# Attention and non-local block: where the sums of the nested products run, and in which order image 0 is prepared

## The chip, the cores and the metric

The kernel runs on one core of one Trainium2 chip. A core has TensorE (matrix products into PSUM, called PE in the profile, with PEld for its weight loads), VectorE (DVE), ScalarE (ACT), GpSimd (POOL), SyncE (SP, which here only issues transfers) and 16 DMA engines. Times are device microseconds (us) of a run; the median over runs is what is compared. The profile is of one more execution.

## The reference

For 8 images x of 512 channels and 32 x 32 positions, in float32:

```
q, k, v = Wq x + bq, Wk x + bk, Wv x + bv          # 1x1 convolutions, 8 heads of 64 channels
attn    = softmax(q^T k / 8)                       # over 1024 keys, per head
x       = x + Wp (attn v) + bp
g, th, ph = Wg x + bg, Wtheta x + btheta, Wphi x + bphi   # 256 channels each
f       = th ph^T / 1024                           # 256 x 256
z       = Ww (f g) + bw + x
out     = (z - mean) * rsqrt(var + 1e-5) * gamma + beta   # per channel, over all images and positions
```

## The kernel before

The function `unshifted` does all the work; `shifted` follows only if a denominator of the softmax is not sane. The channels lie on partitions, in four blocks of 128; an image is a tile of 128 x 4 x 1024.

**Order of the work.** A loop runs over the images b. Its body is: `attention(b)`; then q, v and k of image b+1, in this order, by `heads_of` and `values`; then the projection Wp of image b (`project`); theta and phi (`theta_phi`); and the non-local part (`nonlocal_`: g, f, their product with Ww, z, and the statistics). Image 0's q, k and v come ahead of the loop, in the order q, k, v.

**Products in seven.** Every large product is computed as seven products of half-size blocks in place of eight (a Winograd form). For this the data x = (11, 12; 21, 22) needs sums t1 to t4 (`more_sums`: t1 = 12 - 11, t2 = 22 - t1, t3 = 22 - 12, t4 = 21 - t2) and the weights need sums w3 to w6 (`weight_sums`). `seven` does one such product; its table SEVEN gives each of the seven its weight block, its data block, its PSUM bank and which quarters of the result read it.

**Nested products.** For q, k and v of images 1 to 7 six of the seven outer products are again done in seven (`six`): this needs inner sums of each data block (`inner_parts`, four instructions of 128 x 256 each) and of each weight block (`inner_weights`, kept in DRAM after image 0). The six come as three pairs (SIX): pair 0 gives the quarter 11 and a part of 12, pair 1 gives 22 and a temporary T6, pair 2 a temporary T7 and 21. A pair has seven steps, each with one product for either member. In a step a PSUM bank is read by ACT where the piece is the first of its quarter (`write`), else by DVE, which adds PSUM to the piece in SBUF. The seventh outer product (`plain`, 11 x 11) is done whole between pair 1 and pair 2. ACT copies it to a temporary T1, with the bias, which is then added to T6 and 11. The rest are sums of whole quarters (`add`, 128 x 1024, both operands in SBUF): for q and k, T6 += T1, 11 += T1, 12 += T6, 12 += 22, T7 += T6, 22 += T7, 21 += T7, all on GpSimd; for v two of them on DVE.

**PSUM.** There are four tiles of two banks each; `next_bank` takes the one longest unused. Pair n takes four: two for the products of steps 0, 2, 4 and 6, two for those of steps 1, 3 and 5. The plain product takes one.

**What fills the gaps.** `six` takes `fills`, work of DVE to be put behind a given step of a pair or ("middle") ahead of the plain product. In q these are t3 and t4 of the next image, their inner sums and the softmax's denominators (a reciprocal on DVE, which reads PSUM); in v the four products o x 1/denominator (L677), two on GpSimd and two on DVE; in k the sums t1 to t4 of o (L252) and the inner sums of o's quarter 21; after k those of o's t4. In attention `near_end` puts t1, t2 and four inner sums of x between the steps of the list AT.

**Queues.** `pe`, `dve` and `sp` are one helper, keep_in_program_order: the instruction is placed behind the one written just before it on its engine. Instructions without it are placed by a planner. At run time every engine takes its own in order[...]. So the place of a GpSimd sum in the text orders it against other GpSimd work, not against DVE.

**Image 0.** Its weights come from the inputs; their sums are formed and written to DRAM (`keep`, `keep_inner`). The projection of image 0 is not nested: `weights("WpT")` has no inner sums yet; they are formed after it (L1083), and w3 to w6 of theta/phi in `weights("tp")`. ngamma, dq and dk (differences of biases, used with T7) are formed after q of image 0 (L983 to L986).

Of the kernel before, what the change touches and what calls it, by code (L numbers as in the profile page):

```python
# [8 lines left out]
F32 = mybir.dt.float32  # L9
# [21 lines left out]
def unshifted(ctx: ExitStack, tc: tile.TileContext, a: dict, out: bass.AP):  # L31
# [154 lines left out]
    def weights(name, sums_done=False, pin=lambda ins: None):  # L186

        w = loaded.pop(0)
        assert w.name == name
        if name not in kept:  # L190
            if not sums_done:
                weight_sums(w, corner[name], pin=pin)
            keep("plain" if name == "WpT" else name, w)
        return w
# [51 lines left out]

    def more_sums(data, which, pin=lambda ins: None):
        for i in which:
            l, r = {1: ("12", "11"), 2: ("22", "t1"), 3: ("22", "12"), 4: ("21", "t2")}[i]
            if f"t{i}" not in data:  # L250
                data[f"t{i}"] = block(f"t{i}_{data['name']}")
            pin(nc.vector.tensor_tensor(data[f"t{i}"], data[l], data[r], ALU.subtract))  # L252

# [3 lines left out]

    def inner_parts(data, which, pin=lambda ins: None):
# [5 lines left out]
        return [lambda i=i, l=l, r=r: pin(nc.vector.tensor_tensor(t[:, i], l, r, ALU.subtract))  # L264
                for i, (l, r) in enumerate(((b12, b11), (b22, t[:, 0]), (b22, b12), (b21, t[:, 1])))]
# [85 lines left out]

    def six(name, w, data, positions_out, at, write, fills):

# [19 lines left out]
        def plain():  # L373
            ps = next_bank(f"{name}_0")
            d = data["11"]
            if positions_out:
                ps = ps.rearrange("p h (i f) -> p (h i) f", f=256)
            for i in range(4 if positions_out else 2):
                for k in range(2):
                    if positions_out:  # L380
                        pe(nc.tensor.matmul(ps[:, i, :], d[:, k, i * P:(i + 1) * P], w[:, 0, k, :],  # L381
                                            start=(k == 0 and i % 2 == 0), stop=(k == 1), skip_group_check=True))
                    else:
                        pe(nc.tensor.matmul(ps[:, i, :], w[:, 0, k, i * P:(i + 1) * P], d[:, k, :],
                                            start=(k == 0), stop=(k == 1), skip_group_check=True))
            if positions_out:
                nc.scalar.copy(to("T1"), ps)
            else:
                for i in range(2):
                    write("T1", i, to("T1")[:, i, :], ps[:, i, :])  # L390
            load_w("first")
            add("T6", "T1", nc.vector if positions_out else nc.gpsimd)
            if not positions_out:
                add("11", "T1")
            add("12", "T6")

        for n, pair in enumerate(SIX):
# [7 lines left out]
            for step, which in enumerate(ORDER):  # L405
                _, wi, di, chain, reads = SEVEN[which]
                for m, (outer, of, q) in enumerate(pair):
                    a, d = w.inner(outer)[wi], data[f"inner {of}"][di]
                    ps = slots[m if not chain else 2 + m][:, chain // 2, :256]
                    start = (m, chain) not in begun  # L410
                    begun.add((m, chain))
                    if positions_out:
                        ps = ps.rearrange("p (i f) -> p i f", f=P)
                        for i in range(2):
                            pe(nc.tensor.matmul(ps[:, i, :], d[:, i * P:(i + 1) * P], a, start=start and not i, stop=True,  # L415
                                                skip_group_check=True))
                    else:
                        pe(nc.tensor.matmul(ps, a, d, start=start, stop=True, skip_group_check=True))  # L418
                    for (i, j), is_first in reads:
                        i, j = int(i) - 1, int(j) - 1  # L420
                        if is_first:
                            write(q, i, piece(q, i, j), ps)
                        else:
                            dve(nc.vector.tensor_tensor(piece(q, i, j), piece(q, i, j), ps, ALU.add))  # L424
                for one in fills.pop((n, step), ()):
                    one()
            load_w()
            if n == 1:
                add("12", "22")
        assert not fills, fills  # L430
        if positions_out:
            add("11", "T1", nc.vector)
        add("T7", "T6")
        add("22", "T7")
# [67 lines left out]
    def heads_of(b, what, w, bias, data, pin=lambda ins: None, steps=None, fills=None, **how):  # L502
# [3 lines left out]
        if fills is not None:  # L506
            def write(q, i, to, ps):
                by = steps if q == "T7" else bias if q == "T1" else None
                if by is None:
                    nc.scalar.copy(to, ps)  # L510
                else:
                    nc.scalar.activation(to, ps, AF.Identity, bias=by[:, i:i + 1])

            six(f"p{what}_{b}", w, data, False, lambda q: t[:, rows(q), cols(q)], write, fills)
            return t
# [13 lines left out]
    def values(b, w, data, fills=None):  # L529
# [8 lines left out]
        if fills is not None:  # L538
            six(f"pv_{b}", w, data, True, at, lambda q, i, to, ps: nc.scalar.copy(to, ps), fills)  # L539
            return v  # L540
# [4 lines left out]
    def attention(b, q, k, v, near_end, make_f=None):  # L545
# [128 lines left out]
        def normalize(d):  # L674
# [14 lines left out]
            for k in range(2):  # L689
                for j in range(2):  # L690
                    sp(nc.sync.dma_start(r[j * D:(j + 1) * D, k, :], d[j, k].partition_broadcast(D)))
            r = r.rearrange("q k (p c m) -> q k c p m", p=NPAIR, c=2)
            return [lambda k=k, h=h: product(o["o"][:, :, h * 512 + k * 256:h * 512 + (k + 1) * 256], r[:, k, h],
                                            None if k else nc.gpsimd)
                    for k in range(2) for h in range(NH)]
# [286 lines left out]
    bv, bp, gb, wb, gamma, beta = (load_col(n, nc.sync) for n in ("bvc", "bp", "gb", "Wb", "gamma", "beta"))  # L982
    nc.vector.tensor_scalar(ngamma, gamma, -1.0, 1.0, ALU.mult, ALU.mult)  # L983
    dq, dk = (const.tile([P, CC // 2], F32, tag=n, name=n) for n in ("dq", "dk"))
    for to, of in ((dq, bq), (dk, bk)):
        nc.vector.tensor_tensor(to, of[:, CC // 2:], of[:, :CC // 2], ALU.subtract)  # L986
    weight_sums(wk, corner["WkT"], pin=dve)
# [9 lines left out]
    v = values(0, wv, data)  # L997
    aside_weights = [one for blocks in PAIRS for i in blocks for one in inner_weights(wv, i)]
    held = {}
    AT = (26, 29, *(33 + 8 * n // 5 for n in range(16)))  # L1000
    for b in range(B):
# [6 lines left out]
        if not last:  # L1008
            nxt["data"] = data_sums(quarters_of(nxt["x"]), f"x_{b + 1}", ())
            sums += [lambda i=i: more_sums(nxt["data"], (i,), dve) for i in (1, 2)]  # L1010

# [31 lines left out]
        if not last:  # L1043
            data = nxt["data"]
            t3, t4 = (inner_one_by_one(data, of) for of in ("t3", "t4"))
            q = heads_of(b + 1, "q", weights("WqT"), bq, data, dve, steps=dq, fills={
                (0, 6): [lambda: more_sums(data, (3,), dve)], (1, 0): [lambda: more_sums(data, (4,), dve)],
                (1, 6): t3[:2],
                "middle": [lambda: nxt.update(products=normalize(denominators(next_bank(f"den_{b}")))), *t3[2:], *t4]})
            products = nxt["products"]  # L1050
# [49 lines left out]
        tp = theta_phi(b, weights("tp"), data, tpb, {} if last else  # L1100
                       {5: lambda: b < B - 2 and of_theta.append(f_sums(b, tps[0], 0))})
        load_w("first")
# [247 lines left out]
```

## Time and profile before

Three runs took 2158.82 us at the median (2158.23 to 2159.34). The profiled execution took 2159.93 us; its span, in which instructions ran, is 2158.1 us. The mean clock granted to TensorE is 0.992 of full.

| what | number |
|---|---|
| busy PE / DVE / ACT / POOL, us of 2158.1 | 2105.4 / 1495.6 / 844.2 / 512.2 |
| attention of one image (1142.49 to 1252.51) | 110.02 |
| q, v, then k with the projection (to 1346.70) | 23.50, 22.29, 48.40 |
| theta/phi, then non-local (to 1404.70) | 24.14, 33.86 |
| POOL sum of 128x1024, L371, undisturbed | 2.36 |
| DVE sum of 128x1024, both operands in SBUF, L252 of x | 1.22 |
| the same, L252 of o (t_o), mean of 16 and 16 | 2.05 and 2.16 |
| DVE inner sum of 128x256, L264 of x / of t_o | 0.42 / 1.55 and 2.51 |
| DVE reading PSUM with one SBUF operand: L424 128x256, L603 128x512, L730 128x512 with bias | 0.42, 0.68, 0.74 |
| ACT T1, L512 128x512; T7's first piece, 128x256 | 0.68, 0.48 |

How to read it: a line of the timeline gives the start, the duration, the engine, the line of the kernel, the operation, what it writes and reads, and in brackets how long the engine had been idle and what released it. Ends of matmuls are modelled, and neighbouring ones overlap, so TensorE's gaps are better read from distances between starts. A row of windows gives the stretch, its length, the busy time of PE, PEld, DVE, ACT and POOL with their instructions, the clock granted to TensorE, and the share and rate of the DMA engines.

### The profile page before, as it was taken

Reading aid. Unit: us, or ns where it says so; the run is one execution under the profiler, and the core shown is the slowest. Engines: PE = TensorE matmul, PEld = TensorE weight load, DVE = VectorE, ACT = ScalarE, POOL = GpSimd, SP = SyncE. Lnnn points to the kernel's source line nnn. Section 1 sums busy time; section 2 is a strip of 40 time slices with the busy share of each in tenths; the row PEclk is TensorE's granted clock in tenths of the full one; section 3 lists DMA queues with packets and bytes.
Section 4 is the critical chain, followed back from the end, with each engine's and each line's share of the span. In section 5 each row is a group of like instructions: output and inputs, shape, how many; then the busy total and the mean of one; then the engine's idle time right before and its main releaser. Section 6 shows DMA issues by size and latency. Waiting matters only on the chain.

```text
span 2158.1 us, 33299 instructions
## 1 busy us (share of the span) xinstructions
PE 2105.4 (98%) x13486; PEld 1175.5 (54%) x13486; DVE 1495.6 (69%) x1935; ACT 844.2 (39%) x1220; POOL 512.2 (24%) x340
## 2 busy tenths in 40 slices
PE   9999989999999999999999999999999999999996
PEld 4535754358643577336673376633866348643462
DVE  5587856768677685776857768677684777656736
ACT  1365303653046530464205642066412654056116
POOL 0012800128001370014500155011630117111000
PEclk9999999999999999999999999999999999999998
DMA  6254533235232432325224252142534235212767
GB/s 224 81 143 84 174 123 114 40 79 154 98 108 40 103 126 98 115 38 135 88 98 118 41 152 98 66 123 40 164 122 152 40 57 158 86 30 40 229 221 314
DMA packets 71729, 243.56 MB, mean 113 GB/s; under 512 B 12688, under 2 KB 21136, under 8 KB 69520
## 3 DMA queue, kind: packets, MB, share of 16 engines
q1 hardware_dynamic: 60640, 215.01, 29.9%
q0 software_dynamic: 9072, 24.78, 9.3%
q8 instruction: 108, 1.77, 0.3%
q10 hardware_dynamic: 1856, 1.56, 0.3%
q14 instruction: 53, 0.43, 0.1%
HBM read 160.45 MB, written 47.32 MB: 96 GB/s over the span
## 4 chain that ended last, share of the span: by engine, by line
PE 84%; DVE 9%; DMA 3%; ACT 2%; issue 1%; SPq 0%; ACTq 0%; DVEq 0%; POOLq 0%
PE ps L571 20%; PE po L597 20%; PE ptp L340 8%; PE pv_in L415 6%; PE pq_in L418 5%; PE pp L340 4%; PE pg L340 4%; DVE t_o L252 3%; PE pz L340 3%; DVE i_t_o L264 2%; PE pf L792 2%; PE pp_in_s L297 2%; DVE k L424 1%; PE pv L381 1%; PE pv L340 1%
## 5 line engine op out<-in xcount | busy, mean ns | idle before, releaser
L574 ACT ACTIVATE e<-ps 128x1024 f32<-128x1024 f32 x512 | 523.0, 1025 | 427.5 <-PE ps L571 421.9
L580 DVE TENSOR_TENSOR acc<-acc,e 128x1024 f32<-128x1024 f32 x384 | 469.8, 1223 | 106.6 <-ACT e L574 100.6
L571 PE MATMUL ps<-q,k 64*64 64x512 f32 x4096 | 529.3, 589 | 0.0
L597 PE MATMUL po<-e,v 64*64 64x512 f32 x4096 | 528.6, 589 | 0.0
L610 POOL DMA_DIRECT2D fold<-acc x189 | 144.8, 766 | 1376.4 <-PE ps L571 707.8
L597 PEld LDWEIGHTS po<-e,v 64*64 64x64 f32 x4096 | 156.6, 133 | 282.9 <-issue 275.0
L571 PEld LDWEIGHTS ps<-q,k 64*64 64x64 f32 x4096 | 155.5, 133 | 283.5 <-issue 275.6
L835 ACT ACTIVATE g<-pg,gb 128x512 f32<-128x512 f32 x31 | 21.3, 687 | 467.8 <-PE pg L340 467.6
L578 DVE TENSOR_TENSOR acc<-e,e 128x1024 f32<-128x1024 f32 x64 | 78.3, 1224 | 127.9 <-ACT e L574 125.7
L340 PE MATMUL ptp<-w_tp,t_x 128*128 128x256 f32 x512 | 116.7, 383 | 6.3 <-DVE tp L757 4.6
L340 PEld LDWEIGHTS ptp<-w_tp,t_x 128*128 128x128 f32 x512 | 98.2, 192 | 21.0 <-DVE tp L757 5.4
L340 PE MATMUL pp<-t_o,w_WpT 128*128 128x512 f32 x208 | 103.5, 606 | 0.0
L340 PE MATMUL ptp<-w_tp,x 128*128 128x256 f32 x384 | 86.8, 379 | 0.0
L340 PEld LDWEIGHTS ptp<-w_tp,x 128*128 128x128 f32 x384 | 73.0, 190 | 13.3 <-issue 3.8
L424 DVE TENSOR_TENSOR v<-v,pv_in 128x256 f32<-128x256 f32 x84 | 34.8, 421 | 51.9 <-PE pv_in L415 50.9
L371 POOL TENSOR_TENSOR k<-k,T_pk 128x1024 f32<-128x1024 f32 x28 | 70.1, 2524 | 0.5
L340 PE MATMUL pp<-o,w_WpT 128*128 128x512 f32 x144 | 67.8, 593 | 2.3 <-DVE o L677 2.3
L763 DVE TENSOR_TENSOR tp<-tp,ptp 128x1024 f32<-128x1024 f32 x24 | 29.3, 1221 | 53.5 <-PE ptp L340 53.5
L371 POOL TENSOR_TENSOR q<-q,T_pq 128x1024 f32<-128x1024 f32 x28 | 65.4, 2356 | 0.5
L418 PE MATMUL pk_in<-i_t_x,w_WkT 128*128 128x256 f32 x224 | 57.3, 383 | 2.0 <-DVE k L424 1.2
L510 ACT COPY k<-pk_in 128x256 f32<-128x256 f32 x112 | 42.0, 375 | 44.3 <-PE pk_in L418 40.6
L539 ACT COPY v<-pv_in 128x256 f32<-128x256 f32 x112 | 41.8, 374 | 44.2 <-DVE T_pv L424 19.3
(231 smaller groups left out, 3038.7 us busy)
## 6 DMA issues: line engine op xcount, KB each, us to landing
fold<-acc POOLq DMA_DIRECT2D x189, 128.0 KB, 3.1
w_WqT<-kept_WqT SPq DMA_DIRECT2D x21, 896.0 KB, 4.5
w_WvT<-kept_WvT SPq DMA_DIRECT2D x21, 896.0 KB, 5.1
w_WkT<-kept_WkT SPq DMA_DIRECT2D x21, 896.0 KB, 5.8
r<-den_d SPq DMA_DIRECT2D x32, 512.0 KB, 6.9
x<-in_x_dram SPq DMA_DIRECT2D x30, 512.0 KB, 5.9
spill<-x SPq DMA_DIRECT2D x24, 512.0 KB, 4.0
z<-spill SPq DMA_DIRECT2D x24, 512.0 KB, 10.0
```

Source lines behind the costliest of these rows:

```text
L252: pin(nc.vector.tensor_tensor(data[f"t{i}"], data[l], data[r], ALU.subtract))
L340: pe(nc.tensor.matmul(to_ps, lhsT(k), rhs(k), start=(s, at) not in begun, stop=(k == nk - 1), skip_group_check=True))
L371: dve((engine or nc.gpsimd).tensor_tensor(to(q), to(q), to(of), ALU.add))
L415: pe(nc.tensor.matmul(ps[:, i, :], d[:, i * P:(i + 1) * P], a, start=start and not i, stop=True, skip_group_check=True))
L418: pe(nc.tensor.matmul(ps, a, d, start=start, stop=True, skip_group_check=True))
L424: dve(nc.vector.tensor_tensor(piece(q, i, j), piece(q, i, j), ps, ALU.add))
L571: pe(nc.tensor.matmul(ps[c * P // 2:(c + 1) * P // 2, j, :], k[r, p, keys], q[r, p, h * 512:(h + 1) * 512], start=True, stop=True, skip_gr ...
L574: nc.scalar.activation(e, ps, AF.Exp, scale=SCALE)
L578: nc.vector.tensor_tensor(accs[u], es[u, 0], e, ALU.add)
L580: ins = nc.vector.tensor_tensor(accs[u], accs[u], e, ALU.add)
L597: pe(nc.tensor.matmul(ps[j * D:(j + 1) * D, r, :], v[keys, m, (2 * p + j) * D:(2 * p + j + 1) * D], e[keys, j, :], start=(m == 0), stop=(m ...
L610: nc.gpsimd.dma_start(to, part_of, accum_op=ALU.add)
```

## The change

- `plain` is done in two halves, each in a bank of its own. DVE adds each half straight from PSUM to T6 and to 11 (`plus`, with the bias for q and k). T1 and its ACT copies are gone.
- T7's first pieces are read by DVE as PSUM + T6 (with dq or dk for q and k). T7 += T6 is gone.
- GpSimd has four sums per stage, for v too: 12 += 22 (now written after the plain product), 12 += T6, 22 += T7, 21 += T7.
- All four products o x 1/denominator are GpSimd's. So are o's t1 to t3 (written at the start of k) and the inner sums of o's t4. o's t4 and the inner sums of its 21 stand on DVE after pair 1 of k.
- x's t3 moves into attention, where AT starts at step 22; x's t4 and the inner sums of t3 and t4 stand around pair 1 of q, none in "middle".
- Image 0: dq, dk and ngamma come after v, pinned. Wp's inner sums go between the products of theta/phi, w3 to w5 of theta/phi stand ahead of it and w6 within it; the writes to DRAM and one load come after it.

```diff
@@ weights() @@
-        if name not in kept:
+        if name not in kept and name != "tp":
...
@@ more_sums() and, alike, inner_parts() @@
-            pin(nc.vector.tensor_tensor(data[f"t{i}"], data[l], data[r], ALU.subtract))
+            pin((engine or nc.vector).tensor_tensor(data[f"t{i}"], data[l], data[r], ALU.subtract))
@@ plain() @@
-            ps = next_bank(f"{name}_0")
...
-            if positions_out:
-                nc.scalar.copy(to("T1"), ps)
-            else:
-                for i in range(2):
-                    write("T1", i, to("T1")[:, i, :], ps[:, i, :])
+            for half in range(2):
+                ps = next_bank(f"{name}_0_{half}")[:, 0, :]
...
+                for q in ("T6", "11"):
+                    at_ = to(q)[:, half * 2:half * 2 + 2, :] if positions_out else to(q)[:, half, :]
+                    plus(at_, ps, at_, "first", half)
             load_w("first")
-            add("T6", "T1", nc.vector if positions_out else nc.gpsimd)
-            if not positions_out:
-                add("11", "T1")
+            add("12", "22")
             add("12", "T6")
@@ the pairs @@
-                        if is_first:
-                            write(q, i, piece(q, i, j), ps)
+                        if is_first and q == "T7":
+                            plus(piece(q, i, j), ps, piece("T6", i, j), "third", i)
+                        elif is_first:
+                            nc.scalar.copy(piece(q, i, j), ps)
...
-            if n == 1:
-                add("12", "22")
         assert not fills, fills
-        if positions_out:
-            add("11", "T1", nc.vector)
-        add("T7", "T6")
         add("22", "T7")
         add("21", "T7")
@@ heads_of() @@
+            def plus(to, ps, of, what, i):
+                by = bias if what == "first" else steps
+                dve(nc.vector.scalar_tensor_tensor(to, ps, by[:, i:i + 1], of, ALU.add, ALU.add))
@@ values() @@
-            six(f"pv_{b}", w, data, True, at, lambda q, i, to, ps: nc.scalar.copy(to, ps), fills)
+            six(f"pv_{b}", w, data, True, at, lambda to, ps, of, *_: dve(nc.vector.tensor_tensor(to, of, ps, ALU.add)), fills)
@@ normalize() @@
-                                            None if k else nc.gpsimd)
+                                            nc.gpsimd)
@@ image 0, after q and after v @@
-    nc.vector.tensor_scalar(ngamma, gamma, -1.0, 1.0, ALU.mult, ALU.mult)
-    dq, dk = (const.tile([P, CC // 2], F32, tag=n, name=n) for n in ("dq", "dk"))
...
+        dve(nc.vector.tensor_tensor(to, of[:, CC // 2:], of[:, :CC // 2], ALU.subtract))
+    dve(nc.vector.tensor_scalar(ngamma, gamma, -1.0, 1.0, ALU.mult, ALU.mult))
@@ the loop @@
-    AT = (26, 29, *(33 + 8 * n // 5 for n in range(16)))
+    AT = (22, 25, 28, *(32 + 8 * n // 5 for n in range(16)))
...
-            sums += [lambda i=i: more_sums(nxt["data"], (i,), dve) for i in (1, 2)]
+            sums += [lambda i=i: more_sums(nxt["data"], (i,), dve) for i in (1, 2, 3)]
...
-                (0, 6): [lambda: more_sums(data, (3,), dve)], (1, 0): [lambda: more_sums(data, (4,), dve)],
-                (1, 6): t3[:2],
-                "middle": [lambda: nxt.update(products=normalize(denominators(next_bank(f"den_{b}")))), *t3[2:], *t4]})
+                (0, 6): [lambda: more_sums(data, (4,), dve), t3[0]], (1, 0): t3[1:], (1, 6): t4,
+                "middle": [lambda: nxt.update(products=normalize(denominators(next_bank(f"den_{b}"))))]})
...
-            o_sums = [lambda i=i: more_sums(nxt["o"], (i,), dve) for i in range(1, 5)]
+            o_sums = [lambda i=i: more_sums(nxt["o"], (i,), dve, None if i == 4 else nc.gpsimd) for i in range(1, 5)]
...
-                (0, 6): o_sums[:1], (1, 0): o_sums[1:2], (1, 6): o_sums[2:], "middle": more})
+                (0, 0): o_sums[:3], (1, 6): [*o_sums[3:], *more]})
             if b:
-                inner_sums(nxt["o"], "t4", dve)
+                for one in inner_parts(nxt["o"], "t4", dve, nc.gpsimd):
+                    one()
...
         project(b, xt, o, w, between, nxt.get("o"))
         if b == 0:
-            for i in INNER:
-                for one in inner_weights(w, i):
-                    one()
-            kept["WpT"] = dict(kept["plain"])
-            keep("WpT", w, (0,))
+            w_p = w
         load_w("first")
-        load_w(times=3)
+        load_w(times=3 if b else 2)
...
+        w = weights("tp")
+        between = {} if last else {5: lambda: b < B - 2 and of_theta.append(f_sums(b, tps[0], 0))}
+        if b == 0:
+            weight_sums(w, corner["tp"], (3, 4, 5), dve)
...
+            between.update({1: lambda: weight_sums(w, corner["tp"], (6,), dve), 2: lambda: nest_p(1), 3: lambda: nest_p(2)})
+        tp = theta_phi(b, w, data, tpb, between)
+        if b == 0:
+            keep("tp", w)
+            kept["WpT"] = dict(kept["plain"])
+            keep("WpT", w_p, (0,))
+            load_w()
```

More of the change, by code (lines that the diff above doesn't have):

```diff
@@ L245, in data_sums, with more_sums @@
         return data
-    def more_sums(data, which, pin=lambda ins: None):
+    def more_sums(data, which, pin=lambda ins: None, engine=None):
         for i in which:
@@ L256, in inner_sums, with inner_parts @@
             one()
-    def inner_parts(data, which, pin=lambda ins: None):
+    def inner_parts(data, which, pin=lambda ins: None, engine=None):
         d, name = data[which], f"{which}_{data['name']}"
@@ L263, in inner_parts @@
         data[f"inner {which}"] = {"11": b11, "21": b21, "22": b22, **{f"t{i + 1}": t[:, i] for i in range(4)}}
-        return [lambda i=i, l=l, r=r: pin(nc.vector.tensor_tensor(t[:, i], l, r, ALU.subtract))
+        return [lambda i=i, l=l, r=r: pin((engine or nc.vector).tensor_tensor(t[:, i], l, r, ALU.subtract))
                 for i, (l, r) in enumerate(((b12, b11), (b22, t[:, 0]), (b22, b12), (b21, t[:, 1])))]
@@ L350, in unshifted, with six @@
     ORDER = (0, 1, 2, 5, 4, 3, 6)
-    def six(name, w, data, positions_out, at, write, fills):
+    def six(name, w, data, positions_out, at, plus, fills):
         fills = dict(fills)
@@ L373, in plain @@
         def plain():
-            ps = next_bank(f"{name}_0")
             d = data["11"]
-            if positions_out:
-                ps = ps.rearrange("p h (i f) -> p (h i) f", f=256)
-            for i in range(4 if positions_out else 2):
-                for k in range(2):
-                    if positions_out:
-                        pe(nc.tensor.matmul(ps[:, i, :], d[:, k, i * P:(i + 1) * P], w[:, 0, k, :],
-                                            start=(k == 0 and i % 2 == 0), stop=(k == 1), skip_group_check=True))
-                    else:
-                        pe(nc.tensor.matmul(ps[:, i, :], w[:, 0, k, i * P:(i + 1) * P], d[:, k, :],
-                                            start=(k == 0), stop=(k == 1), skip_group_check=True))
-            if positions_out:
-                nc.scalar.copy(to("T1"), ps)
-            else:
-                for i in range(2):
-                    write("T1", i, to("T1")[:, i, :], ps[:, i, :])
+            for half in range(2):
+                ps = next_bank(f"{name}_0_{half}")[:, 0, :]
+                if positions_out:
+                    ps = ps.rearrange("p (i f) -> p i f", f=256)
+                for i in range(2 if positions_out else 1):
+                    for k in range(2):
+                        if positions_out:
+                            at = (half * 2 + i) * P
+                            pe(nc.tensor.matmul(ps[:, i, :], d[:, k, at:at + P], w[:, 0, k, :],
+                                                start=(k == 0 and i == 0), stop=(k == 1), skip_group_check=True))
+                        else:
+                            pe(nc.tensor.matmul(ps, w[:, 0, k, half * P:(half + 1) * P], d[:, k, :],
+                                                start=(k == 0), stop=(k == 1), skip_group_check=True))
+                for q in ("T6", "11"):
+                    at_ = to(q)[:, half * 2:half * 2 + 2, :] if positions_out else to(q)[:, half, :]
+                    plus(at_, ps, at_, "first", half)
             load_w("first")
-            add("T6", "T1", nc.vector if positions_out else nc.gpsimd)
-            if not positions_out:
-                add("11", "T1")
+            add("12", "22")
             add("12", "T6")
@@ L427, in six @@
             load_w()
-            if n == 1:
-                add("12", "22")
         assert not fills, fills
-        if positions_out:
-            add("11", "T1", nc.vector)
-        add("T7", "T6")
         add("22", "T7")
@@ L506, in heads_of @@
         if fills is not None:
[L507 to L514, printed above, removed]
+            def plus(to, ps, of, what, i):
+                by = bias if what == "first" else steps
+                dve(nc.vector.scalar_tensor_tensor(to, ps, by[:, i:i + 1], of, ALU.add, ALU.add))
+            six(f"p{what}_{b}", w, data, False, lambda q: t[:, rows(q), cols(q)], plus, fills)
             return t
@@ L982, in unshifted @@
     bv, bp, gb, wb, gamma, beta = (load_col(n, nc.sync) for n in ("bvc", "bp", "gb", "Wb", "gamma", "beta"))
-    nc.vector.tensor_scalar(ngamma, gamma, -1.0, 1.0, ALU.mult, ALU.mult)
-    dq, dk = (const.tile([P, CC // 2], F32, tag=n, name=n) for n in ("dq", "dk"))
-    for to, of in ((dq, bq), (dk, bk)):
-        nc.vector.tensor_tensor(to, of[:, CC // 2:], of[:, :CC // 2], ALU.subtract)
     weight_sums(wk, corner["WkT"], pin=dve)
@@ L998, in unshifted @@
     aside_weights = [one for blocks in PAIRS for i in blocks for one in inner_weights(wv, i)]
+    dq, dk = (const.tile([P, CC // 2], F32, tag=n, name=n) for n in ("dq", "dk"))
+    for to, of in ((dq, bq), (dk, bk)):
+        dve(nc.vector.tensor_tensor(to, of[:, CC // 2:], of[:, :CC // 2], ALU.subtract))
+    dve(nc.vector.tensor_scalar(ngamma, gamma, -1.0, 1.0, ALU.mult, ALU.mult))
     held = {}
-    AT = (26, 29, *(33 + 8 * n // 5 for n in range(16)))
+    AT = (22, 25, 28, *(32 + 8 * n // 5 for n in range(16)))
     for b in range(B):
@@ L1099, in unshifted, with nest_p @@
         of_theta = []
-        tp = theta_phi(b, weights("tp"), data, tpb, {} if last else
-                       {5: lambda: b < B - 2 and of_theta.append(f_sums(b, tps[0], 0))})
+        w = weights("tp")
+        between = {} if last else {5: lambda: b < B - 2 and of_theta.append(f_sums(b, tps[0], 0))}
+        if b == 0:
+            weight_sums(w, corner["tp"], (3, 4, 5), dve)
+            def nest_p(i):
+                for one in inner_weights(w_p, i):
+                    one()
+            between.update({1: lambda: weight_sums(w, corner["tp"], (6,), dve), 2: lambda: nest_p(1), 3: lambda: nest_p(2)})
[5 more added lines that the diff above has]
+            load_w()
         load_w("first")
```

## The prediction

> **What bounds the kernel now.** I read the engine totals first, then the chain that ended last, then windows by stage, then the timeline of single stages. Totals and chain:
>
> ```profile
> PE 2105.4 (98%) x13486; PEld 1175.5 (54%) x13486; DVE 1495.6 (69%) x1935; ACT 844.2 (39%) x1220; POOL 512.2 (24%) x340
> ...
> PE 84%; DVE 9%; DMA 3%; ACT 2%; issue 1%; SPq 0%; ACTq 0%; DVEq 0%; POOLq 0%
> ```
>
> TensorE is the bound, so only its gaps can be won. Start-to-start pitches give its pure work: 0.4295 us for a record of 512 columns (eight in 3.43), 0.2156 for 256 columns, 0.1116 for 128 columns where weight loads limit. The product stages of q, k and v are written as three pairs of nested products with seven steps each, the plain product standing before the third pair. With these pitches, attention (110.0), v (22.3), theta/phi (24.2) and the non-local part of an image hold no gap; q, k, the projection and image 0 do. Windows of q, v, k and projection in one image:
>
> ```profile
> 1252.51:1276.01 23.50, 23.44 (x111) 17.84 (x111) 15.10 (x30) 10.24 (x26) 9.85 (x7) 1.00 0.60 148
> 1276.01:1298.30 22.29, 22.29 (x185) 21.87 (x185) 14.79 (x22) 9.66 (x26) 19.33 (x8) 1.00 0.63 195
> 1298.30:1322.00 23.70, 23.56 (x96) 17.73 (x96) 21.11 (x29) 10.44 (x27) 16.94 (x7) 1.00 0.30 96
> 1322.00:1346.70 24.70, 22.28 (x67) 12.35 (x66) 18.35 (x25) 0.00 (x0) 8.48 (x4) 1.00 0.28 89
> ```
>
> By first records, k runs 1298.14 to 1320.60 (22.46; work 84 x 0.2156 + 8 x 0.4295 = 21.55), the projection to 1346.50 (25.9; work 40 x 0.4295 + 28 x 0.2156 = 23.2). The timeline says why:
>
> ```profile
> 1310.73 2.95 POOL L371 TENSOR_TENSOR k<-k 128x1024 f32<-128x1024 f32 x1 [4.77 <-ACT k L510]
> 1311.39 3.37 DVE L252 TENSOR_TENSOR t_o<-o,t_o 128x1024 f32<-128x1024 f32 x1
> ...
> 1330.06 0.70 PE L297 MATMUL pp_in_s<-i_o,w_WpT 128*128 128x256 f32 x2 [2.42 <-DVE x L446]
> ```
>
> A DVE sum (first column start, second duration) takes 3.37 instead of 1.22 while a GpSimd sum (2.36 alone) runs. The i_t_o sums go the same way (2.56 instead of 0.42, from 1325.79); the projection's PSUM reads queue behind them and TensorE waits 2.42. Image 0:
>
> ```profile
> 11.25 0.16 DVE L986 TENSOR_TENSOR dq<-bq 128x2 f32<-128x2 f32 x1 [9.31 <-DMA bq<-in_bq_dram]
> ...
> 16.11 0.69 DVE L107 TENSOR_TENSOR w_early<-a_WkT,w_early 128x512 f32<-128x512 f32 x1 [2.65 <-DMA w_early<-in_WkT_dram]
> ...
> 18.69 5.21 PE L340 MATMUL pq<-t_x,w_WqT 128*128 128x512 f32 x8 [2.40 <-DVE t_x L979]
> ...
> 300.89 5.41 PE L340 MATMUL ptp<-w_tp,t_x 128*128 128x256 f32 x16 [4.36 <-DVE tp L757]
> ```
>
> ```profile
> 302.00:303.00 1.00, 1.00 (x4) 0.79 (x3) 1.00 (x1) 0.00 (x0) 0.00 (x0) 0.50 0.94 284
> ```
>
> Twice DVE waits for a transfer (the second time 5.06, for tp's weights, until 299.01), TensorE after it, and then TensorE runs at half clock (the 0.50 of the window of one us) for about 3.3 us, which costs another 1.6 to 1.8.
>
> [...] The trace agrees: 2.36 + 0.2 to 0.3 for the blocked ones, and PSUM reads beside GpSimd sums at their usual 0.41. It also shows that a waiting GpSimd sum goes ahead of DVE's next one (1310.73 above ran before the t_o of 1311.39). [...] 4.36 idle halved it, 2.42 at 1330 did not, 2.40 at 18.69 did.
>
> **Start.** dq, dk and ngamma move behind v of image 0 and are pinned, so DVE no longer waits for bq; the Wk sums, which were pinned only behind dk and so stood in the middle of the first sums, fall behind q. The second sum then starts when its corner block lands (10.5 in the chain, not 12.11), and the fourth product's operands follow without the 16.11 wait: about 12.5 for w, and the last x part (issued 8.3, landing 3.6 to 6.4 later) plus 1.2 for t. TensorE goes 11.9, 15.3, then 15.3 to 15.9 for the product that began at 18.69, and the next starts at 18.8 to 19.4 instead of 23.73: **-4.6** (-4 to -5). Wk sums and the 24 nested Wq sums slide to 31 to 39.5; k needs w3 at 32.9 and its first DVE add at 43, so they stay hidden.
>
> **Image 0's theta/phi** takes 287.59 to 319.95 = 32.36 against 24.17 in image 1: 8.2 too long. Before, SP held tp's last transfer behind a write that waited for the nested Wp sums (291.58), and DVE did those eight sums (2.44) first. Now the eight go between later products, the write to the end, and the transfer needs only a freed buffer (277 to 281), landing by 286. The moved writes (three of tp, one of Wp) stand on SP's queue ahead of the next Wq and Wv loads only, which are needed 110 us later. Left over: three tp sums (0.6 each) and two x sums (1.13 each) from 289.1 on; s1t1 waits for w3 until about 292 instead of 291.0: 0.9. **-7.3** (-5 to -8.2).
>
> **q.** The plain product now is evicted by four DVE instructions (128x512 with one SBUF operand: 0.744, pitch 0.66; the row exists as L730) instead of two ACT ones (0.684), and T7's four first reads move from ACT (0.48) to DVE (0.48). Both are queued behind the reciprocal (pitch 1.67), and that behind the four t4 parts. GpSimd's first sum (12 += 22) depends only on the second pair, so it still arrives at 1265.06, wherever it stands in the text:
>
> ```profile
> 1265.03 0.42 DVE L264 TENSOR_TENSOR i_t_x<-t_x,i_t_x 128x256 f32<-128x256 f32 x1
> ...
> 1265.06 2.61 POOL L371 TENSOR_TENSOR q<-q 128x1024 f32<-128x1024 f32 x1 [2.62 <-DVE i_t_x L264]
> ...
> 1266.07 1.76 DVE L648 RECIPROCAL fold<-den 128x256 f32<-128x256 f32 x1 [0.61 <-PE den L637]
> ```
>
> Before, the reciprocal (no second SBUF input) covered it. Now the third t4 part stands there and blocks until 1268.0; the fourth ends 1268.3, the reciprocal 1270.0, the four evictions start at 1269.9, 1270.6, 1271.2, 1271.9 and end at 1272.6, the first T7 read at 1273.0. The third pair's step 1 needs the plain product's two banks and step 2 the T7 read: step 2 starts 1273.1 instead of 1271.1 unstalled, 2.0 late; today's wait there (ACT, T1) is 0.4. So +1.6 in five images; image 0's tiny bp addition is blocked there already (+0.75), image 6 waits for a fold transfer anyway (+0.4): **+9.2** (0 to 11; 0 if t4 is not blocked, since then the step waits 0.4 as today).
>
> **v.** Same evictions at 0.68 (L603), DVE free before them because the products go to GpSimd: second half's two end 1.5 after the plain product, one bank 0.2 late. 7 x 0.2 = **+1.4** (0 to 3). The four products on GpSimd (9.4) end about 3.3 before v does.
>
> **k and projection.** From v's end GpSimd runs 22 and 21 += T7 and three o sums, 5 x 2.34 = 11.7, so it ends at 11.9 of k. DVE's t4 of o stands ready at 11.85, ends 13.0; 12 += 22 has waited since 12.3 and takes 13.0 to 15.35; four i_o parts end at 16.7; four evictions at 18.0 (first bank) and 19.3. Step 1 should start at 16.36: first half 1.7 late, second 0.9 more. k = 21.55 + 2.6 = 24.1 (+1.7). Without the block it would be 22.0. Then the i_t_o sums are GpSimd's (done by 32, needed at 38), DVE is free and the projection takes its 23.2 (-2.7). Net -1.0 x 6; image 0 has Wp sums in place of i_o, and no nested projection: +0.15. **-5.9** (-20 to +6).
>
> t3 in attention adds 1.2 to DVE's 84 of 110; x lands by 371 where step 22 is at 392: nothing, under cover of TensorE's own pace (a score buffer waits for DVE only when DVE is some three steps of 1.72 behind; that would cost up to 1.2 per image). ACT's relief is off the path: nothing.
>
> **Sum**: -4.6 - 7.3 + 9.2 + 1.4 - 5.9 = **-7.2**. On the profiled execution (span 2158.1, own time 2159.93) 2150.9 and 2152.7; on the median of 2158.82, 2151.6. About 0.2% (4.3 us) is what a measurement here can tell.
>
> **Rivals.**
> (1) The evictions are not held up: GpSimd's 12 += 22 comes later[...]. For: the change's aim. Against: 1310.73. Without q's block 2142, without k's (7 x 2.1 = 15) 2137. Chance 0.25.
> (2) Slower: GpSimd becomes the bound. Its queue is 11.7 long against 11.85 in k; one sum (2.35) later, each image pays that before the evictions: 7 x 2.35 = 16, giving 2168; it beats today from 1.0 us of delay per image on. Against: 3.3 us of slack inside v. A halved clock in k's waits (1.65 each, 7 times) gives 2163 in the same place; today's 2.42 never does it. Chance 0.15.
> (3) Image 0's edits do nothing, because the tp transfer or the last x part still lands late: 2163 if neither works, 2157 if half does. Chance 0.1.
> The main case has 0.5, its own range 2146 to 2158.
>
> Faster: 0.40 of the main, all of case 1: 0.65. Slower: 0.12 of case 2, 0.04 of case 3, 0.01 of the main: 0.17. Same: 0.18. Range 2138 to 2163: in below case 1 with k's block gone, up to the halved clock.
>
> **What would show it.** First q without the DVE wait for bq, its fifth product near 19; theta/phi of image 0 near 25; in q a t4 part (L264) of about 2.6 beside GpSimd's first sum, and TensorE about 2 us late in the third pair; in k an i_o part of 2.6 and 2.6 of waits; no i_t_o on DVE and no 2.42 in the projection. Wrong if the third pairs of q and k show no waits, or if GpSimd's o sums end after the second pair of k.

## The result and the profile after

The changed kernel takes 2152.85 us (median of 8 runs, 2151.44 to 2154.6); the kernel before 2159.08 (8 runs, 2157.92 to 2161.24). The ratio is 0.997 with an interval of 0.9959 to 0.9981: 6.2 us faster. The forecast was 2151.6, or 7.2 faster. The profiled execution took 2154.6, the longest of the eight, with a span of 2152.8, against 2159.93 and 2158.1.

Engine totals and the chain that ended last, from the page of the kernel after:

```profile
PE 2104.2 (98%) x13486; PEld 1176.3 (55%) x13486; DVE 1444.1 (67%) x2030; ACT 792.4 (37%) x1101; POOL 478.8 (22%) x350
...
PE 90%; DVE 6%; ACT 1%; DMA 1%; issue 1%; DVEq 0%; ACTq 0%; SPq 0%
```

DVE, ACT and GpSimd all have less to do, by 52, 52 and 33 us; TensorE's busy time moved by 1.2. The next view lists what TensorE waited for in the kernel after: who, for whom, us in total, how often, the longest.

```profile
PE pk_in L416 <- DVE k L504: 15.1, 14, 2.0
PE pq_in L416 <- DVE q L504: 6.9, 12, 0.6
PE pp L340 <- DVE o L669: 2.0, 1, 2.0
```

The same view of before was led by the projection:

```profile
PE pp_in_s L297 <- DVE x L446: 14.5, 6, 2.4
PE ptp L340 <- DVE tp L757: 4.6, 2, 4.4
PE pq L340 <- DVE t_x L979: 2.4, 1, 2.4
```

All three waits of before are gone, and two new ones stand in the third pairs of k and q, mostly two in a stage. The lengths of all stages, taken from the first matmul of each to that of the next in both traces, say where the 5.3 us of span went (the right column, which sums to 5.2). Stages are named by the image whose attention ran before them, as in the prediction:

| stage | before | after | change in all |
|---|---|---|---|
| first q, at the start | 29.39 | 24.38 | -5.0 |
| theta/phi of image 0 | 32.36 | 24.28 | -8.1 |
| q, images 0 to 6 | 23.40 to 24.50 | 24.96 to 25.04 | +8.8 |
| v, images 0 to 6 | 22.29 | 22.58 | +2.0 |
| k, images 0 to 6 | 22.47, in image 0 24.40 | 24.25 or 25.9 | +17.1 |
| projection, images 1 to 6 | 25.9 or 27.5 | 23.21 | -20.9 |
| last image, projection and theta/phi | 51.30 | 52.18 | +0.9 |

Attention (110.03) and the rest are unchanged to 0.13 each.

DVE and GpSimd in q of the kernel after, by the timeline (start, duration):

```profile
1256.54 0.42 DVE L264 TENSOR_TENSOR i_t_x<-t_x,i_t_x 128x256 f32<-128x256 f32 x1
1256.56 2.61 POOL L371 TENSOR_TENSOR q<-q 128x1024 f32<-128x1024 f32 x1 [2.76 <-DVE i_t_x L264]
1256.88 2.58 DVE L264 TENSOR_TENSOR i_t_x<-t_x 128x256 f32<-128x256 f32 x1
1259.38 0.41 DVE L264 TENSOR_TENSOR i_t_x<-t_x,i_t_x 128x256 f32<-128x256 f32 x1
1259.71 1.75 DVE L640 RECIPROCAL fold<-den 128x256 f32<-128x256 f32 x1
1261.38 0.65 DVE L504 SCALAR_TENSOR_TENSOR T_pq<-pq,bq,T_pq 128x512 f32<-128x512 f32 x1
...
1263.27 0.74 DVE L504 SCALAR_TENSOR_TENSOR q<-pq,bq,q 128x512 f32<-128x512 f32 x1
```

The GpSimd sum is 12 += 22, 2.61 us long. The third t4 part stands in it for 2.58 instead of 0.42, and everything behind it on DVE (fourth part, reciprocal, four evictions, that is, the reads that empty the PSUM banks) is 2.2 late. The same in k of the kernel after, with GpSimd's sum and TensorE:

```profile
1303.32 1.25 DVE L252 TENSOR_TENSOR t_o<-o,t_o 128x1024 f32<-128x1024 f32 x1
1303.80 2.98 POOL L371 TENSOR_TENSOR k<-k 128x1024 f32<-128x1024 f32 x1 [0.30 <-ACT k L422]
1304.49 2.56 DVE L264 TENSOR_TENSOR i_o<-o 128x256 f32<-128x256 f32 x1
...
1309.56 0.70 PE L416 MATMUL pk_in<-i_t_x,w_WkT 128*128 128x256 f32 x2 [1.53 <-DVE k L504]
1310.88 2.12 PE L416 MATMUL pk_in<-i_t_x,w_WkT 128*128 128x256 f32 x6 [0.62 <-DVE k L504]
```

The i_o part is held up by the same GpSimd sum, and TensorE waits 1.53 and 0.62 for the evictions. The last line shows a second loss: six matmuls in 2.12, where q's six after its wait took 1.56. The clock was halved from 1311.74 to 1315.15, as the windows of one us of the kernel after show (the third number from the end is TensorE's granted clock):

```profile
1312.00:1313.00 1.00, 1.00 (x4) 0.82 (x3) 0.48 (x1) 0.00 (x0) 0.67 (x1) 0.50 0.08 16
```

That happened in four of the seven k stages: 25.9 in images 1, 4 and 6, 25.81 in image 0. In the kernel before it had happened too, in the projection of images 3, 5 and 6 (27.4 to 27.6 instead of 25.9). A window of before shows the first of them:

```profile
1066.00:1068.00 2.00, 1.81 (x3) 1.14 (x4) 0.89 (x3) 0.00 (x0) 0.70 (x1) 0.57 0.00 0
```

So the forecast's sentence that "today's 2.42 never does it" was wrong: it rested on one image.

### The profile page after: what moved, and what is told of

It reads as the page before. It is cut to its first block, busy times and chain, and to the rows that moved or that the text cites. A ratio compares the mean times of both kernels' runs of the same rounds, so it can differ in the third digit from the quotient of the medians.

```text
span 2152.8 us, 33275 instructions
## 1 busy us (share of the span) xinstructions
PE 2104.2 (98%) x13486; PEld 1176.3 (55%) x13486; DVE 1444.1 (67%) x2030; ACT 792.4 (37%) x1101; POOL 478.8 (22%) x350
## 3 DMA queue, kind: packets, MB, share of 16 engines
q8 instruction: 108, 1.77, 0.3%
q10 hardware_dynamic: 1856, 1.56, 0.3%
## 4 chain that ended last, share of the span: by engine, by line
PE 90%; DVE 6%; ACT 1%; DMA 1%; issue 1%; DVEq 0%; ACTq 0%; SPq 0%
PE ps L563 20%; PE po L589 20%; PE ptp L340 9%; PE pp L340 7%; PE pv_in L413 6%; PE pq_in L416 5%; PE pk_in L416 5%; PE pg L340 4%; PE pz L340 3%; PE pf L784 2%; PE pp_in_s L297 2%; PE pv L383 1%; PE pv L340 1%; PE pk L340 1%; PE pwf L839 1%; ACT z L959 1%
## 5 line engine op out<-in xcount | busy, mean ns | idle before, releaser
L422 ACT COPY q<-pq_in 128x256 f32<-128x256 f32 x112 | 41.7, 373 | 119.4 <-PE pq_in L416 116.0
L416 PE MATMUL pk_in<-i_t_x,w_WkT 128*128 128x256 f32 x224 | 62.4, 410 | 15.1 <-DVE k L504 15.1
L424 DVE TENSOR_TENSOR v<-v,pv_in 128x256 f32<-128x256 f32 x84 | 34.8, 421 | 50.8 <-PE pv_in L413 48.4
L424 DVE TENSOR_TENSOR k<-k,pk_in 128x256 f32<-128x256 f32 x84 | 35.4, 421 | 48.0 <-PE pk_in L416 45.9
L669 POOL TENSOR_TENSOR o<-o,r 128x1024 f32<-128x1024 f32 x28 | 65.2, 2363 | 0.0
```

What stands on the lines that cost most here:

```text
L422: nc.scalar.copy(piece(q, i, j), ps)
L669: dve((engine or nc.vector).tensor_tensor(at, at, of, ALU.mult))
```

## The experiments

**Theory A**, that of the forecast: the waits in the third pairs come from DVE's sums of two SBUF operands (t4 parts in q, i_o in k), which are blocked by GpSimd's 12 += 22; the evictions queue behind them. **Theory B**: DVE simply has too much queued there, and the block is incidental. **Theory C**: the halved clock makes the size. A and B part where DVE keeps its work and its order, and GpSimd alone does its first two sums the other way round. The experiments ran in three groups, each with runs of the kernel before beside it (medians 2159.87, 2158.47 and 2158.84), and the ratios are to these; so 1 us or so between medians of different groups says nothing. Lengths of stages are those of each kernel's one profiled execution.

### The two GpSimd sums exchanged, everywhere

```
-            add("12", "22")
             add("12", "T6")
+            add("12", "22")
```

> The changed kernel with GpSimd's first two sums of a product stage exchanged: 12 += T6 stands ahead of 12 += 22. The first of them then has to wait for DVE's evictions of the plain product, so that no GpSimd sum runs while DVE does its two-operand sums (t4 parts in q, i_o parts in k); DVE's own work and order stay as they are. Theory A (these sums are blocked by 12 += 22, and the evictions behind them come late): i_t_x and i_o parts of 0.42, no waits left in the third pair of k and less than 0.3 in that of q; q 24.96 -> 23.4 to 23.8, k 24.24 or 25.9 -> 22.0 to 22.2, and no halved clock; 6 in q and 21 in k, median about 2126. Theory B (DVE simply has too much queued there, four evictions and four T7 reads): q, k and the median as they are, 2153. Theory C (only the halved clock in four of k's stages makes the size): about 6, 2147.

Measured: 2126.85 (2124.58 to 2127.55), ratio 0.9848 to before (0.9835 to 0.9862), 26.0 below the changed kernel. q is 23.61 to 23.65 in images 1 to 5 (24.65 in image 0, 24.18 in image 6), k 22.13 to 22.16 (22.6 in image 0), the projection 23.21. What TensorE waits for in this kernel:

```profile
PE pk_in L416 <- DVE k L504: 2.5, 7, 0.6
PE pp L340 <- DVE o L669: 1.9, 1, 1.9
PE pq_in L416 <- DVE q L504: 1.9, 7, 0.3
```

22.0 us of waits have become 4.4. k of this kernel by its timeline:

```profile
1286.73 1.30 DVE L252 TENSOR_TENSOR t_o<-o,t_o 128x1024 f32<-128x1024 f32 x1
...
1287.95 0.41 DVE L264 TENSOR_TENSOR i_o<-o 128x256 f32<-128x256 f32 x1
1288.40 0.42 DVE L264 TENSOR_TENSOR i_o<-o,i_o 128x256 f32<-128x256 f32 x1
...
1291.55 2.35 POOL L371 TENSOR_TENSOR k<-k,T_pk 128x1024 f32<-128x1024 f32 x1 [4.60 <-DVE T_pk L504]
```

The first i_o part takes 0.41, not 2.56, and GpSimd stands idle for 4.60 until T6 has both halves; 12 += 22, now second in the text, waits behind. DVE's count of instructions is that of the changed kernel (2030), its busy time 27.5 lower (1416.6 against 1444.1). In the changed kernel 14 sums of DVE are held up by 2.14 to 2.16 each, one in every q and every k, 30.1 in all; in this one none is. B falls, since no work was taken from DVE. C falls as a full account: not 6 but 26 was won; that the halved clocks of k went too (the mean granted clock of the profiled executions rose from 0.992 to 0.995) follows from A, as they had come after its waits.

### The exchange in q alone, and in k alone

```
-            add("12", "22")
-            add("12", "T6")
+            for of in ("T6", "22") if name.startswith("pq") else ("22", "T6"):
+                add("12", of)
```

and the same with "pk".

> The same exchange in q alone. Theory A: q 24.96 -> 23.4 to 23.8, k as it is (24.24 or 25.9), median about 2147. Theory B: no change, 2153. If GpSimd's queue is so full that a later start of its sums moves into v and k, k gets longer by up to 2.3 per image and the median rises.

> The same exchange in k alone. Theory A: k 24.24 or 25.9 -> 22.0 to 22.2 in all images, q as it is (24.96), projection still 23.2, median about 2132. Theory B: no change. Theory C: k keeps its 2.1 of waits and loses the 1.65 of the four images with a halved clock, 2147.

Measured: in q alone 2145.1 (2143.73 to 2148.86), ratio 0.9932 (0.9917 to 0.9947), 7.8 below the changed kernel; in k alone 2132.58 (2131.97 to 2132.99), ratio 0.9875 (0.986 to 0.9891), 20.3 below it. The two together are 28.0, against 26.0 for both at once. Stage by stage the parts stay apart: with q's exchange q is 23.61 and k stays at 24.2 or 25.9 (the longer form in five stages now, 26.37 in image 0; the profiled execution, 2148.86 with a mean granted clock of 0.991, was the longest of four); with k's, k is 22.11 and q 24.96. GpSimd's later start in q costs v and k nothing. Where the clock had stayed full, k is 2.1 shorter than in the changed kernel, 15 in seven stages; the other 6 of k's 21 is the halved clock of four stages, which is gone from every k (mean granted clock 0.996). So C holds as a part of k's price.

### The edits of image 0 alone

The kernel before with only the moved dq, dk and ngamma and the changed order around theta/phi of image 0:

```
-    for to, of in ((dq, bq), (dk, bk)):
-        nc.vector.tensor_tensor(to, of[:, CC // 2:], of[:, :CC // 2], ALU.subtract)
     weight_sums(wk, corner["WkT"], pin=dve)
...
     v = values(0, wv, data)
...
+    for to, of in ((dq, bq), (dk, bk)):
+        dve(nc.vector.tensor_tensor(to, of[:, CC // 2:], of[:, :CC // 2], ALU.subtract))
...
-        tp = theta_phi(b, weights("tp"), data, tpb, {} if last else
+        tp = theta_phi(b, w, data, tpb, between)
+        if b == 0:
+            keep("tp", w)
```

> The kernel before with the two edits on image 0 alone: dq, dk and ngamma behind v of image 0, and the order of tp's and Wp's sums, nested sums and writes around theta/phi. If they do what the prediction's steps say: first q 29.39 -> about 24.4 from the span's start, theta/phi of image 0 32.36 -> about 24.3, everything else as before, so 13.1 faster than before: about 2146. If the gain depends on the other edits (a transfer that lands late without them), half of it or less. The rest of the change then is worth the difference to 2153: about +7 slower than these edits alone.

Measured: 2146.38 (2145.31 to 2147.99), ratio 0.9941 (0.9926 to 0.9957), 13.5 faster than before. First q 24.40 long, theta/phi of image 0 24.17. The gain doesn't need the other edits. The rest of the change, taken as it was made, cost 6.5: 2146.4 to 2152.85. With the two sums exchanged (2126.85) the same rest brings 19.5.

### DVE's sums moved from under the GpSimd sum

If A is right, q must win the same when GpSimd keeps its order and DVE's two-operand sums come earlier:

```
-    AT = (22, 25, 28, *(32 + 8 * n // 5 for n in range(16)))
+    AT = (22, 25, 28, 30, *(32 + 8 * n // 5 for n in range(16)))
...
-                (0, 6): [lambda: more_sums(data, (4,), dve), t3[0]], (1, 0): t3[1:], (1, 6): t4,
+                (0, 6): t3, (1, 0): t4,
```

> The changed kernel with GpSimd's order as it is (12 += 22 first), but with DVE's work taken from under it in q: the fourth sum of x moves into attention (step 30) and all eight t3 and t4 parts stand between the first and the second pair of q, so that DVE has no two-operand sum left when 12 += 22 starts. Theory A: q 24.96 -> 23.6 as with the exchange in q, k as it is, median about 2147. Theory D[...]: q stays at 24.96, 2153. If the added sum holds attention up, attention gets longer by up to 1.2 per image.

> Both: the exchange of GpSimd's two sums in every stage and the earlier sums of x. Theory A: nothing is left to win in q, since in both ways no DVE sum meets a GpSimd sum any more: q 23.6, median 2127 (within 2). If the rest of q (23.6 over 21.55 of products and 1.07 of denominators) still is DVE queueing in front of the reciprocal, q falls to 23.0 or less and the median to 2123.

Measured: without the exchange 2145.1 (2144.16 to 2150.62), ratio 0.9933 (0.9914 to 0.9952), with q at 23.61 and attention at 110.03; with it 2124.75 (2124.47 to 2126.46), ratio 0.984 (0.9822 to 0.9858), q again 23.61. Two edits that share nothing but the removed meeting of a DVE and a GpSimd sum give the same 1.35 per stage, and together no more. Theory D, that 12 += T6 helped by coming earlier, falls for q; in k, where more was won, no such second test was made, and the timeline above stands for it. With both edits q stays at 23.61 and does not fall to 23.0, so a queue of DVE in front of the reciprocal is not what is left. Without the exchange k keeps its waits (15.4 us), four of its seven stages run into the halved clock, and image 0's is 27.67; that profiled execution, 2150.62 with a mean granted clock of 0.99, was again the longest of its runs. The 1.2 that the fourth sum adds to attention's DVE costs nothing. The two exchanged versions, 2126.85 and 2124.75, have overlapping intervals; both beat the changed kernel and the one before.

### What is left in q, v and k

q is 0.22 and v 0.29 longer than before. In the next kernel the second half of the plain product is not added to 11 (that part of the result is missing):

```
-                for q in ("T6", "11"):
+                for q in ("T6", "11") if half == 0 else ("T6",):
```

> The exchanged order, and the second half of the plain product is added to T6 alone: its addition to 11 is left out (in q, k and v), which leaves that part of the result out. Its bank then comes free one DVE eviction (0.6 to 0.67) earlier. If what is left of the lengthening in v (22.58 against 22.29) and in q (23.61 against 23.39) is that bank coming free late: v 22.3, q 23.4, k 21.9, median 2122 to 2123. If it is the splitting of the plain product over two banks: no change, 2127.

Measured: 2114.32 (2114.08 to 2116.02): v 22.21, q 23.06, k 21.57, and no wait of TensorE for an eviction of q, v or k is left. The eviction is worth more than v's and q's lengthening showed: 0.54 per q, 0.36 per v, 0.58 per k, 10.2 in all (1.5 of the 12.5 is the last image, whose projection ran at full clock here, 1.00 in the windows from 1985 to 1989, and in the kernel compared with at 0.50 from 1997 to 1999). But leaving it out does two things at once: the bank comes free one eviction earlier, and so do T7's reads, which stand behind it on DVE (the first at 17.96 of q, at 18.62 in the exchanged kernel). This run doesn't tell them apart. Two ways of freeing the bank alone were tried. In the first, DVE adds the second half to T6 while ACT copies it, in q and v:

```
+                if shared:
+                    plus(spare, ps, None, "first", half)
...
+            dve(nc.gpsimd.tensor_tensor(at_, at_, spare, ALU.add))
```

> The exchanged order, and in q and v the second half of the plain product is read by two engines at once: DVE adds it to T6 while ACT copies it to a spare buffer, from which GpSimd adds it to 11 after its first two sums (half of 2.35 more on its queue per stage, under 3.4 of slack there). If the late bank is the cause: v 22.3, q 23.4, k as it is (22.15), median about 2123.5. If GpSimd's queue then reaches into k, k gets up to 1.2 longer per image and the gain is lost: 2127 to 2131.

In the second, ACT alone reads the bank, in q, v and k, and then in q and v only:

```
+                if copied:
+                    plus(at_("T1"), ps, None, "first", half)
+                    dve(nc.vector.tensor_tensor(at_("T6"), at_("T6"), at_("T1"), ALU.add))
...
+                dve(nc.gpsimd.tensor_tensor(at_("11"), at_("11"), at_("T1"), ALU.add))
```

> The exchanged order, and in q, v and k the second half of the plain product is read only once, by ACT, into a spare buffer; DVE then adds that buffer to T6 (a sum of two SBUF operands of 128x512, while GpSimd is idle), GpSimd adds it to 11 after its first two sums (half of 2.35 more on its queue). The bank then comes free after one read of 0.58 to 0.69 instead of two DVE reads (1.4). If the bank's last read is what the third pair waits for: q 23.1 to 23.3, v 22.25, k 21.6 to 21.8, 8 in all, median 2116 to 2119. If the sum into T6, which stands ahead of T7's first reads on DVE, takes the bank's place as what comes late: no change, 2124 to 2127. If GpSimd's queue gets too long: k up by 1.2 per image.

> The same in q and v only, k as in the exchanged order (22.15). If the late bank is the cause: about 5 in all, median 2119 to 2122. The difference to the version with k tells whether GpSimd's longer queue in k costs anything: 3 to 4 faster with k if not, slower with k if so.

Measured, in this order: 2124.49 (2124.02 to 2126.07), 2124.27 (2123.12 to 2126.73) and 2128.95 (2127.87 to 2132.96), ratios 0.9841 (0.9822 to 0.986), 0.9845 (0.9829 to 0.9861) and 0.9868 (0.9852 to 0.9884). The first comes near its 2123.5, but not by q and v, which were to fall to 23.4 and 22.3; the second and third miss the 2116 to 2119 and 2119 to 2122 of a late bank. They win at most 0.1 per q and 0.15 per v: q 23.67, 23.51 and 23.51, v 22.53, 22.43 and 22.43. k is 22.26, 22.19 and 22.93, and of the first two's 2.4 below the exchange 1.6 is the last image's clock again: after the wait there eight matmuls of 512 columns took 3.70 in either, as they did at the clock of 1.00 with one eviction less. In the first, ACT's copy did not run beside DVE's read of the bank:

```profile
1245.83 0.75 DVE L515 SCALAR_TENSOR_TENSOR T_pq<-pq,bq,T_pq 128x512 f32<-128x512 f32 x1 [0.38 <-PE pq L386]
...
1246.62 0.69 ACT L513 ACTIVATE T_pq<-pq,bq 128x512 f32<-128x512 f32 x1 [5.12 <-DVE T_pq L515]
```

It started 0.04 after the end of that read and released the bank as late as a second DVE read would. The bracket names that read as what released ACT: the copy waited for it by the program, so this run doesn't tell whether both could read at once. In q of the other two, the sum into T6 takes the bank's place, as the second branch of the expectation said: TensorE then waits for a T7 read (pq_in for T_pq, 1.2 in all; the first of these reads starts at 18.56 of q, hardly earlier than 18.62). So q is held by DVE's queue, whichever engine empties the bank. The third is also a measurement of GpSimd's queue, which is longer by a sum of 1.28 in v, with k's own work unchanged. Its timeline in k:

```profile
1288.79 2.12 DVE L252 TENSOR_TENSOR t_o<-o,t_o 128x1024 f32<-128x1024 f32 x1
1290.83 0.41 DVE L264 TENSOR_TENSOR i_o<-o 128x256 f32<-128x256 f32 x1
```

GpSimd's last o sum ended at 1289.82, 12.87 after k's first matmul; in the exchanged kernel it ended at 12.06. DVE's t4 sum stood behind it for 0.8 longer, and k is 0.8 longer (22.93 for 22.15). The other 0.5 of the longer queue was slack in v.

The second kernel has the same longer queue, and in its k the t4 sum is held up just as long:

```profile
1285.62 2.13 DVE L252 TENSOR_TENSOR t_o<-o,t_o 128x1024 f32<-128x1024 f32 x1
```

Yet its k is 22.19, 0.74 shorter than the third's. So in k the copy by ACT did win, 0.74 per image, about 5 in seven stages, where the two medians, 2124.27 and 2128.95, lie 4.7 apart, and the late sum of GpSimd took 0.8 of it back. What both expectations put as alternatives happened together.

## Why the prediction was right, and where it was off

The time was within 1.3 us. The steps:

- **Start, -4.6 forecast, -5.0 measured.** The fifth product began at 18.63 (forecast "near 19"), without a wait for a sum of x.
- **Theta/phi of image 0, -7.3 forecast, -8.1 measured.** The 0.9 "left over" didn't come. Counted from the start of the stage (287.59 before, 284.73 after), the product that needs the first of tp's three sums was to begin at about 4.4 and began at 3.5, without a wait: the two sums of x that the forecast put in front of it had started at -1.3 and 0.2, not from 1.5 on.
- **q, +9.2 forecast, +8.8 measured.** The step is confirmed nearly to the digit: +1.56 in four images and +1.23 in one where +1.6 was worked out, +0.54 in the first for +0.75, +0.76 in the last for +0.4. The blocked t4 part, 2.6 by forecast, is 2.58.
- **v, +1.4 forecast, +2.0 measured.** 0.29 per image for 0.2. That the last eviction is behind it shows where it is left out (v 22.21, below the 22.29 of before); the bank alone is not shown.
- **k and projection, -5.9 forecast, -3.9 measured.** Where the clock stayed full, k lengthened by 1.77 (forecast 1.7) and the projection shortened by 2.69 (forecast 2.7). Two terms were mis-sized. In image 0, k was to lose 0.15 and lost 1.4: the Wp sum of 128x512 that stands in i_o's place was blocked just the same, 2.83 instead of 0.69, and TensorE waited 1.98 and 0.26, with a halved clock after it (253.61 to 257.02). And the halved clock was taken as something that the waits of before did not cause: they did in three images (1.5 to 1.7 each, won back by the change), and those of after in four stages. Together these put 6.7 more on k than forecast and took 4.7 more off the projection. That the two nearly cancel in the total was not forecast, and is luck.
- **The last image, +0.9**, had no step. The wait for the o products, 2.29 before and 2.02 after, is nothing of the change; after the shorter of the two the clock was halved (0.50 from 2025.12 to 2028.53) and after the longer it was not (1.00 from 2030 to 2033); the last section shows where the two fell.

The rivals: (1) was not what happened, but its price is now measured: without q's block the forecast said 2142 and the runs 2145.1, without k's 2137 and 2132.6; k's is higher since its waits also halved the clock. (2), a late GpSimd queue, did not decide: 12 += 22 waited 0.30 for ACT in k, not for GpSimd's own earlier sums. Its price, one for one, shows in the last experiment: 0.8 later is 0.8 longer. The part of (2) with a halved clock came true in four of seven stages. (3) fell: both edits of image 0 do what they say.

The steps of q and k rested on what the trace of before showed of DVE beside GpSimd, and the kernel after shows the same. Its 14 DVE sums of two SBUF operands that were held up took 2.56 to 2.58 (128x256) and 2.83 (128x512) instead of 0.42 and 0.69, and ended 0.28 and 0.55 after the GpSimd sum beside them. That sum was longer too, 2.60 to 2.98 where it takes 2.36 alone. DVE's reads of PSUM with one SBUF operand kept their length beside GpSimd's sums: 0.41 to 0.42 for 128x256 (L424), 0.73 to 0.74 for 128x512 with bias (L504). So did the reciprocal of before, 1.76 for 1.74. What in the chip makes two such sums hold each other up was not shown.

## What to carry to other kernels

When sums are spread over two engines and hold each other up, as here (2.58 for 0.42 on DVE, 2.61 for 2.36 on GpSimd), the order on the engine with slack can decide what the other's critical work costs: let the slack engine's first sum be the one that depends on the critical work, so that it cannot start in front of it. Here that exchange of two lines was worth 26 us, four times the whole change. Before a cost is put at "it does not happen here", look at that place in every image: the halved clock was there in three of six.

## What the runs showed of the hardware

A wait of TensorE of about 2 us was followed by a halved clock in some executions of the same stage and not in others: in the kernel before in the projection of images 3, 5 and 6 (27.4 to 27.6 long, 25.9 in the other three); in k in four stages of the changed kernel (images 0, 1, 4, 6: 25.8 to 25.9 long, 24.25 in the other three) and in five with q's exchange (0, 2, 4, 5, 6: 25.9 and 26.37, 24.2 in the others). By the lengths with and without it, it cost 1.5 to 1.7 us each time. The forecast's 4.36 and 2.40 (halved) and 2.42 (not halved) are waits of TensorE as well.

In these traces the length of the wait alone did not tell the two apart; where it fell did. In the changed kernel the halved stretches of k and of the last image begin at 253.61, 519.85, 1311.74, 1827.15 and 2025.12, and each lasts 3.41: the later four lie 266.24, 1058.13, 1573.54 and 1771.51 behind the first, which is 78, 310, 461 and 519 times 3.413. In the kernel before five such stretches begin at 18.37, 301.68, 1066.26, 1591.91 and 1844.50, the later four 83, 307, 461 and 535 times 3.413 behind the first. So each of the two traces can be divided into stretches of that length. Here are two of them in k of image 3, which stayed at full clock, then two in k of image 4, which didn't (the number behind the length is TensorE's busy time, the third from the end its granted clock):

```profile
1042.09:1045.50 3.41, 2.84 (x9) 1.33 (x7) 3.38 (x5) 0.37 (x1) 1.57 (x1) 1.00 0.30 72
1045.50:1048.91 3.41, 1.84 (x7) 1.29 (x8) 2.99 (x6) 0.37 (x1) 1.71 (x1) 1.00 0.18 64
1308.33:1311.74 3.41, 1.56 (x6) 1.04 (x7) 3.28 (x6) 0.24 (x2) 1.43 (x1) 1.00 0.22 70
1311.74:1315.15 3.41, 3.41 (x10) 2.71 (x9) 1.31 (x3) 0.62 (x2) 0.93 (x1) 0.50 0.02 5
```

The waits of k, about 2.15 together, are split 0.57 and 1.57 over two stretches in the first stage; in the second 1.85 falls into one, and the next runs at half clock. In these two traces, from the first record of the clock (4.43 after, 4.72 before) to the last product, TensorE stood idle for 1.85 to 2.63 us of the stretch ahead of each of the ten halved ones. In every other stretch at full clock it was idle for 1.84 (from 800.02 in the kernel before) or less. That fits the last image: the wait of 2.29 before was split 0.51 and 1.78, and that of 2.02 after fell into one stretch. So, as an estimate from these numbers, a change that shifts a later stage by a microsecond can win or lose 1.6 there. What sets the stretches was not shown.
